# A fused AdaLN block on one core: the pass over x written out as a software pipeline on every engine

## The chip, the core and the metric

The kernel runs on one core of a Trainium2 chip. The metric is the device time of one execution in microseconds. A core has five engines that run beside each other, each with its own queue that it works through in order: TensorE (PE, matrix products, with its weight loads shown as PEld), VectorE (DVE), ScalarE (ACT), GpSimd (POOL) and SyncE (SP), which here issues nearly all DMAs. Engines wait for each other through semaphores. An instruction that waits at the head of a queue holds all that stands behind it on that engine.

## What is computed

With x of shape (2, 2048, 1024), and a modulation vector of six parts (sa, ca, ga, sb, cb, gb) for each of the two batch rows:

```
h = layernorm(x) * (1 + ca) + sa
q = h with the 2048 tokens as the reduced axis; for each of the 1024 channels l:
    scores[n, m] = sum over tokens of h[n, token, l] * h[m, token, l] / sqrt(2048)   (2 x 2)
    msg = softmax(scores) @ q
x = x + ga * (h + msg)
h = layernorm(x) * (1 + cb) + sb
x = x + gb * (silu(h @ Wg.T) * (h @ Wu.T)) @ Wd.T        (1024 -> 2752 -> 1024)
```

The modulation is silu(c) @ wmod with wmod of 1024 x 6144. Since the scores need sums over all 2048 tokens, the whole of x must be read once before the first token can go on: that reading is the pass over x that is changed here. With z = (x - mean) * r, where r is one over the standard deviation, the pass forms for each channel the five sums of z0, z1, z0², z1² and z0·z1 (0 and 1 are the batch rows).

## The kernel before

**The stages.** (1) The pass over x: eight sections of 256 tokens, both batch rows. (2) A short stage in which the sums become the 2 x 2 softmax and the modulation parts 2 to 4 are formed. (3) Eight units of 256 tokens each, which redo the normalisation for their tokens and run the feed-forward network. The products of stage 3 are split into f16 high and low parts.

**A section in the pass.** A section has four blocks of 128 tokens x 1024 channels, block (n, c) for batch row n and token half c. `x_load` (line 232) brings each row's two blocks by one DMA of 1 MB. There are eight such places in SBUF, so section s + 4 goes where section s was, and its load waits until all readers of section s are done. `x_stats` (line 245) runs `bn_stats` on half blocks and `bn_aggr` per block on DVE (lines 255 and 256), a square root on ACT (line 122), five small dependent DVE instructions (lines 125 to 128 and 261), and writes the columns r/D and nb/D of row 0 into `lw`, a weight tile of PE (line 263; nb = -mean·r, D = 1024). `x_sums` (line 287) forms z of row 1 (block c = 0 on GpSimd, line 296, and c = 1 on ACT, line 294), takes row 0 straight from x with `lw` as the weights, has the squares done by ACT (lines 315 and 316) and the mixed product by GpSimd (line 312), and adds everything up in the PSUM tile `sums` by fp32 products of 32 columns (line 299). Because row 0 is not centred in the mixed product, a product with a column of ones (`one`, line 325) corrects it. Each `add` call has a column group of 32; four of them, with four different groups, run beside each other on PE.

**Beside the sections.** For section 0, z of both rows is kept in `z_first` (in the tile `H`), and `x_turn` (line 274) transposes x and z of section 0 on PE, block of 128 channels by block, through the PSUM tile `pz`, with the copies out of PSUM taken in turn by ACT (line 285) and DVE (line 283). Parts 0 and 1 of the modulation are formed by `section_of` (line 193): four loads of 1 MB, sixteen products (line 167), a copy on ACT (line 173), four small turning products (line 176), and a copy on DVE (line 183).

**What sets the order.** Only SP is in the order of the program text (line 1036). On PE, DVE, ACT and GpSimd a list scheduler chooses the order in each queue from modelled costs; all waits between engines follow from the data. In the queues that it built, the eight `x_turn` copies of z stand among the sums of sections 0 to 2, and the statistics of a section run one to two sections ahead of its sums. After the pass, `srow` (line 1079) copies the sums out and four products `pq` (line 1081) turn them.

Of the kernel before, what the change touches and what calls it, by code (L numbers as in the profile page):

```python
# [8 lines left out]
F32 = mybir.dt.float32  # L9
F16 = mybir.dt.float16  # L10
# [7 lines left out]
P = 128  # L18
# [29 lines left out]
def adaln_kernel(ctx, tc, x, xT, wgp, wg20, wgl, wd, wd20, wd21, wmod, cT, out, nunits=NU):  # L48
# [11 lines left out]
    def ct(shape, name, dt=F32):  # L60
        return const.tile(shape, dt, tag=name, name=name)
# [13 lines left out]
    def xtile(u):  # L75
        return big[:, u % 2].rearrange("p (k n c) -> p k n c", k=KB, n=2)
# [5 lines left out]
    pick = ct([P, 34], "pick")  # L82
    V.memset(pick, 0.0)
    V.memset(pick[:, 2:3], 1.0 / D)
    one = ct([P, 1], "one")
    V.memset(one, 1.0)
    epst = ct([P, 1], "epst")
    V.memset(epst, EPS)

# [29 lines left out]
    def rsqrt(dst, v, shape, pool, tag):  # L119

        s = pool if tag is None else pool.tile(shape, F32, tag=tag, name=tag + "s")
        first = S.activation(s, v, AF.Sqrt, bias=epst)
        n = shape[-1]
        for o in range(0, n, P):
            V.reciprocal(dst[:, o:min(n, o + P)], s[:, o:min(n, o + P)])
        V.scalar_tensor_tensor(s, v, EPS, dst, ALU.add, ALU.mult)
        V.scalar_tensor_tensor(s, s, -0.5, dst, ALU.mult, ALU.mult)
        return first, V.scalar_tensor_tensor(dst, s, 1.5, dst, ALU.add, ALU.mult)
# [29 lines left out]
    def mod_load(j, kk, slots):  # L158
        wm = slots[kk % len(slots)]
        last_load[0] = Q.dma_start(wm, wmod[2 * kk * P:(2 * kk + 2) * P, j * D:(j + 1) * D].rearrange("(k p) e -> p k e", p=P))  # L160
        return wm

    def mod_mul(pm, kk, wm):
        for i in range(2):
            for h in range(2):
                o = 32 * (2 * i + h)
                last = T.matmul(pm[o:o + 32], csT[:, 2 * kk + i], wm[:, i, h * 512:(h + 1) * 512],
                                start=kk == 0, stop=kk == KB // 2 - 1, skip_group_check=True)
        return last

    def mod_end(j, pm, tag):
        row = evp.tile([P, 512], F32, tag="ev", name=f"row{j}", bufs=3)
        S.copy(row, pm)
        pt = ps.tile([P, KB // 2, 2, 2], F32, tag=tag, name=f"pt{j}")
        for k in range(KB // 2):
            mark["turn", j] = T.matmul(pt[:, k], row[:, k * P:(k + 1) * P], sel, start=k == 0, stop=k == KB // 2 - 1,
                                       skip_group_check=True)
        m = mods[j] = ct([P, KB, 2], f"mod{j}")
        m = m.rearrange("p (h k) n -> p k h n", h=2)
        if j == 4:  # L180
            V.tensor_single_scalar(m, pt, 1.0, ALU.add)
        else:
            V.tensor_copy(m, pt)
# [9 lines left out]
    def section_of(j, wms, tag, after=None):  # L193

        pm = ps.tile([P, 512], F32, tag=tag, name=f"pm{j}")
        for kk, wm in enumerate(wms):
            with tc.issue_after(after[kk].ins) if after else ExitStack():
                mod_mul(pm, kk, wm)
        mod_end(j, pm, tag)
# [16 lines left out]
    stat = dr.tile([NU, 2, 2, TU], F32, tag="stat", name="stat")  # L216
    mods = {}
    NC = TU // P
    toks = ct([P, NU, 2, 2, NC], "toks")


# [4 lines left out]
    def z_tiles(s):  # L226
        return x_tiles(s) if s else z_first

    def x_tiles(s):
        return [xnat[(2 * s + n) % len(xnat)] for n in range(2)]  # L230

    def x_load(s):
        for n in range(2):
            Q.dma_start(x_tiles(s)[n], x[n, s * TU:(s + 1) * TU, :].rearrange("(c p) e -> p c e", p=P))

    lw = tmp.tile([P, 2 * TU], F32, tag="acc", name="lw", bufs=1)[:, 0:4 * NC * 34]
    V.memset(lw, 0.0)
    lw = lw.rearrange("p (b w c e) -> p b w c e", b=2, w=2, c=NC)  # L240
    V.memset(lw[:, :, 1, :, 0:1], 1.0 / D)
    nbs = ct([P, 2, 2, NC], "nbs")
    zz_at = [hpf, bct.rearrange("p a n c -> p (a n c)")]

    def x_stats(s):
        xs = x_tiles(s)
        tok = toks[:, s]

        st4 = ps.tile([P, 3 * 2 * NC], F32, tag="X", name="st4")
        mv = st4[:, 0:4 * NC].rearrange("p (n c t) -> p n c t", n=2, c=NC)  # L250
        for n in range(2):
            for c in range(NC):
                st = small.tile([P, 2, 6], F32, tag="bst", name="bst")
                for h in range(2):
                    V.bn_stats(out=st[:, h, :], in_=xs[n][:, c, h * 512:(h + 1) * 512])
                V.bn_aggr(out=mv[:, n, c, :], in_=st)
        r = tok[:, 0].rearrange("p n c -> p (n c)")
        mean, var = (mv.rearrange("p n c t -> p (n c) t")[:, :, t] for t in range(2))
        rsqrt(r, var, [P, 2 * NC], st4[:, 4 * NC:], None)
        nb = nbs[:, s % 2].rearrange("p n c -> p (n c)")  # L260
        V.scalar_tensor_tensor(nb, mean, -1.0, r, ALU.mult, ALU.mult)
        for w, t in enumerate((r, nb)):
            V.tensor_single_scalar(lw[:, s % 2, w, :, 2], t[:, 0:NC], 1.0 / D, ALU.mult)
        V.tensor_single_scalar(tok[:, 1].rearrange("p n c -> p (n c)"), mean, -1.0, ALU.mult)

    def stat_rows():
        n = NU * 4 * NC
# [3 lines left out]
        S.copy(rows, p16[0:n, :])  # L271
        S.dma_start(stat.rearrange("s w n (c p) -> (s w n c) p", p=P), rows)

    def x_turn(dst, src):

        for k in range(KB):
            pz = ps.tile([P, 2, NC, P], F32, tag="Z", name="pz")
            for n in range(2):
                for c in range(NC):
                    T.transpose(pz[:, n, c], src[n][:, c, k * P:(k + 1) * P], ident)  # L280
            d = dst[:, k].rearrange("p n (c t) -> p n c t", c=NC)
            if k % 2:
                V.tensor_copy(d, pz)
            else:
                S.copy(d, pz)

    def x_sums(s):

        xs, zs = x_tiles(s), z_tiles(s)
        tok, nb, lws = toks[:, s], nbs[:, s % 2], lw[:, s % 2]  # L290

        def z_of(n, c):
            if c:
                S.activation(zs[n][:, c], xs[n][:, c], AF.Identity, scale=tok[:, 0, n, c:c + 1], bias=nb[:, n, c:c + 1])
            else:
                G.tensor_scalar(zs[n][:, c], xs[n][:, c], tok[:, 0, n, c:c + 1], nb[:, n, c:c + 1], ALU.mult, ALU.add)

        def add(g, w, src, first=False):
            mark["sums", s] = T.matmul(sums_ps[32 * g:32 * g + 32], w, src, start=first, stop=s == NU - 1,  # L299
                                       skip_group_check=True)  # L300

        for c in range(NC):
            z_of(1, c)
        if s == 0:
            for c in range(NC):
                z_of(0, c)
        zq = {}
        half = lambda t, h: t[:, h * 512:(h + 1) * 512]
        for c in range(NC):
            x0, z1 = xs[0][:, c], zs[1][:, c]  # L310
            zz = zz_at[c]
            G.tensor_tensor(zz, x0, z1, ALU.mult)
            for n in range(2):
                zq[n] = wp.tile([P, 2 * KH * P], F16, tag="w", name="zq").bitcast(F32)[:, 0:D]
            S.activation(zq[0], x0, AF.Square, scale=tok[:, 0, 0, c:c + 1], bias=nb[:, 0, c:c + 1])
            S.activation(zq[1], z1, AF.Square)
            for h in range(2):
                add(h, lws[:, 0, c, 2:34], half(x0, h), s == 0 and c == 0)
            for h in range(2):
                add(2 + h, lws[:, 1, c, 0:32], half(z1, h), s == 0 and c == 0)  # L320
            for n in range(2):
                for h in range(2):
                    add(2 * n + h, pick[:, 1:33], half(zq[n], h))
            for h in range(2):
                add(h, lws[:, 1, c, 2:34], one.broadcast_to([P, 512]))
            for h in range(2):
                add(2 + h, lws[:, 0, c, 0:32], half(zz, h))


    s_gu = ct([P, NP + 2], "s_gu")  # L330
# [703 lines left out]
    pairs = {0: Pair(0, four(H[:, 12:20].rearrange("p a n c -> p (a n c)")))}  # L1034
    in_order = ExitStack()
    in_order.enter_context(tc.manual_schedule(engines={mybir.EngineType.SP}))
    for g in range(4):
        x_load(g)
    wms = [mod_load(0, kk, slots[0:4]) for kk in range(4)]
    x_stats(0)  # L1040
    x_turn(xtile(0), x_tiles(0))
    x_stats(1)
    x_sums(0)
    x_load(4)
    x_turn(zt, z_first)
    for g in range(1, NU):
        if g + 1 < NU:
            x_stats(g + 1)
        x_sums(g)
        if g + 4 < NU:  # L1050
            x_load(g + 4)
        if g == 1:
            section_of(0, wms, "Z")
            wms = [mod_load(1, kk, slots[0:4]) for kk in range(4)]
        if g == 3:
            section_of(1, wms, "Z")
    stat_rows()


# [134 lines left out]
```

## Time and profile before

| | |
|---|---|
| median of 3 runs | 2642.22 us (2641.72 to 2643.38) |
| the profiled execution, own time | 2644.62 us |
| its span in the trace | 2642.8 us |
| PE busy over the span | 2570.5 us, 97% |
| DVE, ACT, POOL busy | 1593.3, 977.2, 125.9 us |
| first transposition on PE | at 9.67 us |
| `pq`, first product after the pass | at 98.48 us |
| PE busy, stretch 168 to 200 and 200 to 300 us | 32.00 of 32.00 and 100.00 of 100.00 us |

Times inside the trace are counted from the start of the span. In a list of instructions a row gives start, duration, engine, line, operation, output <- input, shape and count, and in square brackets how long the engine was idle before it and what ended that idle time. In a table of stretches a row gives the stretch, its length, each engine's busy time (with the number of instructions), the granted TensorE clock as a share of full speed, the DMA share and GB/s.

### The profile page before, as it was taken

How to read it: one execution, taken by the hardware profiler on the slowest of the kernel's cores; microseconds unless marked ns; L12 is line 12 of the kernel's file. 1: busy time of each engine (PE TensorE's matmuls, PEld its weight loads, DVE VectorE, ACT ScalarE, POOL GpSimd, SP SyncE). 2: the span in 40 equal slices, each digit the busy share in tenths (PEclk: the TensorE clock that was granted, in tenths of full speed). 3: DMA queues.
4: the chain of work that ended last, by engine and by line, in shares of the span. 5: the costliest groups of instructions: out<-in, count | busy, mean ns of one | idle time of the engine just before them, and what ended most of it. 6: DMA issues, size and time to landing. Idle time of an engine off the chain costs nothing.

```text
span 2642.8 us, 50765 instructions
## 1 busy us (share of the span) xinstructions
PE 2570.5 (97%) x21737; PEld 2089.9 (79%) x21737; DVE 1593.3 (60%) x2666; ACT 977.2 (37%) x1488; POOL 125.9 (5%) x71
## 2 busy tenths in 40 slices
PE   7899989999999999999999999999999999999999
PEld 2344448778888888878887888878887888888887
DVE  7567779866684877584384725684284824622263
ACT  5666764433441454243241423333142412311130
POOL 4311100000000000000000000000000000000000
PEclk8899999999999999999999999999999999999999
DMA  8978775565567776576666666566666666556664
GB/s 320 356 281 305 295 276 192 199 221 198 170 204 268 262 250 205 194 236 201 186 218 217 212 200 199 198 237 201 192 208 208 218 200 202 200 194 201 202 200 152
DMA packets 159011, 586.62 MB, mean 222 GB/s; under 512 B 17217, under 2 KB 17281, under 8 KB 158785
## 3 DMA queue, kind: packets, MB, share of 16 engines
q1 hardware_dynamic: 158704, 583.35, 64.8%
q8 instruction: 170, 2.79, 0.4%
q14 instruction: 57, 0.46, 0.1%
q10 hardware_dynamic: 80, 0.03, 0.0%
HBM read 506.47 MB, written 76.84 MB: 221 GB/s over the span
## 4 chain that ended last, share of the span: by engine, by line
PE 78%; DMA 9%; DVE 7%; ACT 3%; issue 2%; SPq 0%; POOL 0%; DVEq 0%; ACTq 0%; POOLq 0%
PE pY L790 19%; PE pZ L790 12%; PE pX L790 12%; PE dY L994 11%; PE dX L994 8%; PE dZ L994 7%; PE pB L1020 2%; PE g L758 2%; PE sums L299 2%; PE pl L828 1%; DMA wo<-dgu 1%; DMA out_dram<-big 1%; ACT junk L117 1%; DMA rot<-in_wgp_dram 1%; PE g L733 1%
## 5 line engine op out<-in xcount | busy, mean ns | idle before, releaser
L790 PEld LDWEIGHTS <-w 128*128 128x128 f16 x8820 | 860.7, 98 | 108.4 <-DMA w<-dgu 4.9
L994 PEld LDWEIGHTS <-wd 128*128 128x128 f16 x6720 | 657.8, 98 | 84.1 <-DMA wd<-dwd 4.0
L790 PE MATMUL pY<-hbt,w 128*128 128x256 f16 x3780 | 442.4, 273 | 0.0
L994 PE MATMUL dY<-rot,wd 128*128 128x256 f16 x2880 | 320.3, 274 | 0.0
L790 PE MATMUL pX<-hbt,w 128*128 128x256 f16 x2520 | 300.6, 273 | 0.0
L790 PE MATMUL pZ<-hbt,w 128*128 128x256 f16 x2520 | 294.5, 273 | 3.8 <-DMA w<-dgu 3.7
L790 PEld LDWEIGHTS <-wo 128*128 128x128 f16 x2688 | 263.4, 98 | 41.1 <-DMA wo<-dgu 5.6
L134 ACT ACTIVATE rot<-H,sA 128x1024 f16<-128x1024 f32 (+1 forms) x168 | 162.7, 1001 | 238.1 <-PE dY L994 129.8
L135 DVE SCALAR_TENSOR_TENSOR rot<-H,sA,rot 128x1024 f16<-128x1024 f32 (+1 forms) x168 | 182.1, 1099 | 78.2 <-ACT rot L134 77.9
L733 PE MATMUL g<-hbt,wq 128*128 128x512 f16 x1008 | 221.0, 379 | 1.8 <-ACT hbt L675 1.2
L994 PE MATMUL dX<-rot,wd 128*128 128x256 f16 x1920 | 212.9, 273 | 6.0 <-DMA wd<-dwd 3.7
L994 PE MATMUL dZ<-rot,wd 128*128 128x256 f16 x1920 | 213.5, 273 | 0.0
L807 DVE TENSOR_TENSOR ev<-pY,e 128x512 f32<-128x512 f32 (+1 forms) x72 | 47.8, 663 | 254.7 <-PE pY L790 253.6
L733 PEld LDWEIGHTS <-wq 128*128 128x128 f16 x1008 | 98.2, 98 | 119.8 <-issue 2.5
L117 ACT ACTIVATE junk<-H 128x1024 bf16<-128x1024 f32 (+1 forms) x100 | 98.7, 987 | 161.9 <-DVE H L817 143.7
L812 ACT ACTIVATE sil<-ev,inv_f 128x512 f32<-128x512 f32 (+1 forms) x72 | 50.5, 701 | 246.3 <-DVE ev L810 246.1
L790 PE MATMUL pY<-hbt,wo 128*128 128x256 f16 x1152 | 135.2, 273 | 3.6 <-DVE ev L807 2.6
L587 ACT ACTIVATE o<-big,beta,alpha 128x256 f32<-128x256 f32 x112 | 59.9, 591 | 207.2 <-DVE big L573 183.6
L798 DVE TENSOR_TENSOR ev<-pY,e 128x512 f32<-128x512 f32 (+1 forms) x72 | 47.7, 662 | 124.1 <-PE pY L790 124.1
L758 PE MATMUL g<-hbt,wo 128*128 128x256 f16 x960 | 108.3, 275 | 3.3 <-DMA wo<-dgu 3.1
L801 ACT COPY e<-pZ 128x512 f32<-128x512 f32 (+1 forms) x72 | 40.3, 560 | 188.5 <-PE pZ L790 188.5
L758 PEld LDWEIGHTS <-wo 128*128 128x128 f16 x960 | 94.4, 99 | 16.2 <-DMA wo<-dgu 3.3
(291 smaller groups left out, 2763.7 us busy)
## 6 DMA issues: line engine op xcount, KB each, us to landing
w<-dgu SPq DMA_DIRECT2D x350, 512.0 KB, 4.2
wd<-dwd SPq DMA_DIRECT2D x224, 640.0 KB, 4.0
wo<-dgu SPq DMA_DIRECT2D x85, 512.0 KB, 5.4
dgu<-wo SPq DMA_DIRECT2D x40, 512.0 KB, 4.0
rot<-in_wgp_dram SPq DMA_DIRECT2D x38, 512.0 KB, 5.8
dgu<-wq SPq DMA_DIRECT2D x35, 512.0 KB, 6.6
big<-in_wgp_dram SPq DMA_DIRECT2D x32, 512.0 KB, 7.5
out_dram<-big SPq DMA_DIRECT2D x30, 512.0 KB, 3.1
```

What stands on the lines that cost most here:

```text
L117: S.activation(jv, src, AF.Square, accum_out=col)
L134: mark["hi"] = S.activation(dst_hi, src, AF.Copy, scale=s)
L135: return V.scalar_tensor_tensor(dst_lo, src, s, dst_hi, ALU.mult, ALU.subtract)
L299: mark["sums", s] = T.matmul(sums_ps[32 * g:32 * g + 32], w, src, start=first, stop=s == NU - 1, skip_group_check=True)
L587: S.activation(o[:, n], z[:, q, 0], AF.Identity, scale=alpha[:, n, 0, q:q + 1], bias=beta[:, n, q:q + 1])
L733: T.matmul(pt[m, f].rearrange("p n c -> p (n c)"), w[:, wa, f, k], hb0[:, ha, 4 * kh + k], start=kh == 0 and k == 0 and j == 0, stop=kh == ...
L758: T.matmul(pt[m, f][:, n], w[:, wa, f, k], hb[:, ((1, 0), (2, 3))[kh][n], ha, k], start=kh == 0 and k == 0 and j == 0 and n == 0, stop=kh ...
L790: T.matmul(pt[a][:, f], w[:, wa, f, k], hb[:, i, ha, k], start=a not in seen, stop=k == 3 and j == 2, skip_group_check=True)
L807: V.tensor_tensor(c22, pt["Y"], e1, ALU.add)
L812: S.activation(sr, u2, AF.Silu, scale=inv)
L994: T.matmul(acc[a, h][:, j], w[:, k // 5, wa, k % 5], rot16[:, si % 2, ha, k], start=(a, h) not in seen, stop=k == KH - 1 and jj == 2, skip ...
L1020: T.matmul(pB, wt[0:n, k, wa, m, :], hp[0:n, k, ha, :], start=i == 0, stop=i == len(LAST) - 1)
```

## The change

1. z is formed for all four blocks of every section: block (0, 0) on DVE, (1, 0) on GpSimd, (0, 1) and (1, 1) on ACT. All sums then have plain z, z² or z·z as data and the constant `pick` as weights. The tile `lw` and its DVE writes, `one` and its products are gone: 20 products per section in place of 24.
2. PE, DVE, ACT and GpSimd are put in the order of the program text for the whole pass (`in_text`). The text is written as a pipeline: step s (`x_step`) holds the statistics of section s + 1 around the z of section s.
3. The transposition of x of section 0 has all eight copies on ACT, ahead of the first square root. The transposition of z is spread out: one channel block after the sums of each of the steps 1 to 7, its copy on ACT after odd steps and on DVE after even ones, and the eighth after the last step.
4. The loads of modulation parts 0 and 1 are issued in halves between the loads of x, and their products stand in halves behind the sums of steps 2 and 3 (part 0) and 5 and 6 (part 1).

The diff, cut to its core (`stats` keeps the `bn_stats` and `bn_aggr` of one row; `root` is the square root on ACT; `squares` two squares on ACT):

```diff
-        for w, t in enumerate((r, nb)):
-            V.tensor_single_scalar(lw[:, s % 2, w, :, 2], t[:, 0:NC], 1.0 / D, ALU.mult)
...
+    def dev(s):
+        mean, v, r = parts(s)
+        d = toks[:, s, 0].rearrange("p n c -> p (n c)")
+        V.reciprocal(d, r)
+        V.scalar_tensor_tensor(r, v, EPS, d, ALU.add, ALU.mult)
+        V.scalar_tensor_tensor(r, r, -0.5, d, ALU.mult, ALU.mult)
+        V.scalar_tensor_tensor(d, r, 1.5, d, ALU.add, ALU.mult)
+        V.scalar_tensor_tensor(nbs[:, s % 2].rearrange("p n c -> p (n c)"), mean, -1.0, d, ALU.mult, ALU.mult)
+        V.tensor_single_scalar(toks[:, s, 1].rearrange("p n c -> p (n c)"), mean, -1.0, ALU.mult)
+
+    def z_of(E, s, n, c):
+        src, dst = x_tiles(s)[n][:, c], z_tiles(s)[n][:, c]
+        r, nb = toks[:, s, 0, n, c:c + 1], nbs[:, s % 2, n, c:c + 1]
+        if E is S:
+            S.activation(dst, src, AF.Identity, scale=r, bias=nb)
+        else:
+            E.tensor_scalar(dst, src, r, nb, ALU.mult, ALU.add)
...
+    def x_turn(dst, src, k, E):
+        pz = ps.tile([P, 2, NC, P], F32, tag="Z", name="pz")
+        for n in range(2):
+            for c in range(NC):
+                T.transpose(pz[:, n, c], src[n][:, c, k * P:(k + 1) * P], ident)
+        d = dst[:, k].rearrange("p n (c t) -> p n c t", c=NC)
+        S.copy(d, pz) if E is S else V.tensor_copy(d, pz)
...
+    def x_step(s):
+        z = [[z_tiles(s)[n][:, c] for n in range(2)] for c in range(NC)]
...
+        if more:
+            stats(s + 1, 0)
+        dev(s)
+        z_of(V, s, 0, 0)
+        if more:
+            stats(s + 1, 1)
+        z_of(G, s, 1, 0)
+        for n in range(2):
+            z_of(S, s, n, 1)
+        for c in range(NC):
+            G.tensor_tensor(zz_at[c], z[c][0], z[c][1], ALU.mult)
+        zq = squares(s, 0)
+        if more:
+            root(s + 1)
+        zq += squares(s, 1)
+        for c in range(NC):
+            for n in range(2):
+                add(s, 0, 2 * n, z[c][n])
+        for n in range(2):
+            add(s, 1, 2 * n, zq[n])
+        for c in range(NC):
+            add(s, 2, 2 * c, zz_at[c])
+        for n in range(2):
+            add(s, 1, 2 * n, zq[2 + n])
...
+    in_text.enter_context(tc.manual_schedule(engines={getattr(mybir.EngineType, e) for e in ENGINES}))
     for g in range(4):
         x_load(g)
-    wms = [mod_load(0, kk, slots[0:4]) for kk in range(4)]
-    x_stats(0)
-    x_turn(xtile(0), x_tiles(0))
...
+    w0 = [mod_load(0, kk, slots[0:4]) for kk in range(2)]
+    stats(0, 0)
+    stats(0, 1)
+    for k in range(KB):
+        x_turn(xtile(0), x_tiles(0), k, S)
+    root(0)
+    for g in range(NU):
+        x_step(g)
         if g + 4 < NU:
             x_load(g + 4)
+        if g == 0:
+            w0 += [mod_load(0, kk, slots[0:4]) for kk in (2, 3)]
+        if g == 2:
+            pm0 = ps.tile([P, 512], F32, tag="st", name="pm0")
+            for kk in range(2):
+                mod_mul(pm0, kk, w0[kk])
+            w1 = [mod_load(1, kk, slots[0:4]) for kk in range(2)]
+        if g == 3:
+            for kk in (2, 3):
+                mod_mul(pm0, kk, w0[kk])
+            mod_end(0, pm0, "st")
+            w1 += [mod_load(1, kk, slots[0:4]) for kk in (2, 3)]
...
+        if g:
+            x_turn(zt, z_first, g - 1, S if g % 2 else V)
+    x_turn(zt, z_first, KB - 1, V)
+    in_text.close()
     stat_rows()
```

Steps 5 and 6 do for part 1 what steps 2 and 3 do for part 0.

## The prediction

> **What bounds the kernel now.** I read the stretches first: from 168 us on PE is busy without a break, so nothing later can take back what the start loses or gains; and of the time that PE waits between 100 and 340 us none goes to a DMA (6.6 us on GpSimd, the rest on ACT and DVE). So a shift of the first product after the pass (`pq`, 98.48 us) goes into the end time one to one. I then followed the chain of waits through the pass:
>
> ```profile
> 74.28 3.47 PE sums L299 x34
> 77.75 1.00 PE pt L176 x8
> ...
> 82.17 7.40 PE sums L299 x32
> ...
> 93.36 4.33 PE sums L299 x42
> 97.69 0.86 PE pm L167 x8
> 98.55 0.99 PE pq L1081 x8
> ```
>
> From 41 us to the end the chain is PE's queue itself, with one break at 78 to 82. Before 41 us it is DVE. What an engine does when its next instruction is not ready shows in DVE's own order of time:
>
> ```profile
> 35.45 1.73 DVE L263 TENSOR_SCALAR lw<-nbs 128x2 f32<-128x2 f32 x1
> 37.10 2.39 DVE L263 TENSOR_SCALAR lw<-toks 128x2 f32<-128x2 f32 x1
> ...
> 42.99 0.16 DVE L261 SCALAR_TENSOR_TENSOR nbs<-st,toks 128x4 f32<-128x4 f32 x1
> 47.65 0.17 DVE L263 TENSOR_SCALAR lw<-toks 128x2 f32<-128x2 f32 x1 [4.50 <-PE sums L299]
> ```
>
> Two things: a write of two elements took 2.39 us while GpSimd ran its 2.34 us product (37.13), against 0.16 elsewhere; and one DVE instruction that needed PE's sums held the whole DVE queue 4.50 us. The second is what I expect of the change. The durations for the sum, by operation, in the pass (mean ns behind the busy time):
>
> ```profile
> L255 DVE BATCH_NORM_STATS2 bst<-hbt 128x6 f32<-128x512 f32 x32 | 19.6, 669 | 0.0
> L312 POOL TENSOR_TENSOR hp<-hbt 128x1024 f32<-128x1024 f32 x3 | 7.2, 2385 | 0.1
> ...
> L316 ACT ACTIVATE zq<-hbt 128x1024 f32<-128x1024 f32 x6 | 6.3, 1043 | 0.0
> ...
> L294 ACT ACTIVATE hbt<-hbt,nbs,toks 128x1024 f32<-128x1024 f32 x3 | 3.7, 1234 | 1.8 <-DVE nbs L261 1.8
> L296 POOL TENSOR_SCALAR hbt<-hbt,toks,nbs 128x1024 f32<-128x1024 f32 x3 | 3.6, 1200 | 3.5 <-DVE lw L263 2.0 <-DVE toks L264 1.6
> ```
>
> Back to back, ACT starts one every 1.13 (z) and 0.95 (square), and DVE a `bn_stats` every 0.60. PE starts eight records, four products in four groups, at 47.40 and the next eight at 48.26: 0.86 a group of four.
>
> **What is removed.** 24 products a section become 20, six groups of four become five: 8 x 0.86 = 6.9 us of PE. The 16 writes of L263 go, 9.9 us of DVE with their blocking. Both are gains only if those engines stay the bound. **What is added:** a z on DVE each section, and seven more on ACT (7 x 1.13, on an engine idle for 45 of the first 100 us: free). The DMAs are the same; x of section 4 is asked for right after the z of section 0, near 24 us in place of 30.67. In the slower pass below loads are ahead by 10 us or more everywhere, so the halved loads cost and bring nothing; the 4.0 us that DVE waited for x at 69 us go.
>
> **The new order.** Per step, from the moment `dev` (the five dependent DVE instructions, 84.63 to 85.68, with the next 1.1) is done:
> - DVE: z of block (0, 0), then half of the next statistics, 4 x 0.60 + 2 x 0.2 + hand-offs = 2.9, then the other half, 2.9, then `dev`, 1.1. The z is not in the trace. Upper bound 1.2, as two-input operations on 1024 elements (L366, 1.22); lower bound 0.6, half of that, as the blocking of L263 behind GpSimd hints that the form uses a second port. I take 0.9, next to the 0.91 of the only DVE row with 1024 fp32 results and no such input (a memset, L496). Period 0.9 + 2.9 + 2.9 + 1.1 = **7.8**.
> - GpSimd: z 1.2 after DVE's, then two products of 2.4: done at 6.9. ACT: two z, two squares, root 0.2, two squares: done at 6.4. PE then has the second mixed product and the last squares, two half-overlapping pairs, 1.6: sums done at **8.5**.
>
> Sums of step s end 8.5 after `dev`, later than DVE's 3.8 for the statistics that it does before the next half section. That is harmless until something on DVE waits for what stands behind the sums on PE. The text puts just that there: after steps 2, 4 and 6 DVE's copy of the transposed z, and after steps 3 and 6 the copy of the modulation part. Behind the waiting copy stand the next statistics (2.9) and `dev` (1.1), and for `dev` all four engines wait. By step, from `dev` to the next `dev`:
> - Steps 0, 1, 5: 7.8 each. After 1 and 5 the copy is on ACT; it ends 9.8 and 11.6 after `dev` (5 has two groups of products, 1.7, ahead), so ACT starts the next step 2.0 and 3.8 late.
> - Step 2: ACT late by 2.0, sums at 9.3; products 1.7; transpositions 0.6 (4 at L280); copy 0.7 (L283); hand-offs 0.2: 12.5. Then 2.9 + 1.1: **16.5**.
> - Step 3: 8.5 + products 1.7 + copy on ACT 0.6 (L173) + turning 1.0 (L176) + copy 0.2 + hand-offs 0.3 = 12.3, + 4.0: **16.3**.
> - Step 4: 8.5 + 0.6 + 0.7 + 0.1 + 4.0 = **13.9**.
> - Step 6: ACT late by 3.8, sums at 11.1; 1.7 + 0.6 + 1.0 + 0.3, transpositions 0.6, copy 0.7 with small DVE work: 16.1, + 1.1: **17.2**.
> - Step 7: 8.5.
>
> The first `dev`: eight copies on ACT in a row, two `pz` buffers, about 0.9 each with transpositions of 1.1 at the low clock, from 11.2 to 18.3; table load 1.28, root 0.24, `dev` 1.1: 20.8 (before 23.1). Sum: 20.8 + 3 x 7.8 + 16.5 + 16.3 + 13.9 + 17.2 + 8.5 = **116.6**.
>
> **The clock.** PE's granted clock (third number from the end of a row; PE's busy time is the second) falls after thin stretches:
>
> ```profile
> 16.50:20.00 3.50, 1.97 (x8) 1.43 (x8) 3.49 (x12) 0.56 (x1) 0.00 (x0) 0.50 1.03 412
> 20.00:23.40 3.40, 1.38 (x6) 0.71 (x4) 3.40 (x13) 0.67 (x2) 0.01 (x1) 0.50 1.02 408
> 23.40:26.70 3.30, 3.29 (x8) 0.41 (x8) 3.27 (x10) 3.30 (x3) 3.30 (x3) 0.51 1.03 408
> 26.70:30.00 3.30, 3.30 (x32) 2.17 (x34) 3.30 (x10) 3.30 (x6) 3.30 (x2) 1.00 1.02 407
> ...
> 36.80:40.10 3.30, 0.01 (x1) 0.00 (x0) 3.30 (x4) 3.30 (x4) 2.66 (x2) 1.00 0.61 245
> 40.10:43.50 3.40, 3.36 (x16) 1.24 (x20) 1.87 (x8) 2.30 (x5) 0.00 (x0) 0.52 0.00 1
> ```
>
> A stretch with PE busy 56% left it at 0.50, one full stretch brought it back, an idle one lost it. Each long step leaves PE idle 4 us or more, so the next one starts at half clock; its first groups have room (they wait for GpSimd and ACT anyway), so I count half of a second 0.86 + 0.6 in each of four steps: 4 x 0.75 = 3.0. Sums end at 119.6, against 97.7 before: **+21.9**.
>
> **After the pass.** Two transpositions now stand ahead of `pq`: 1.2 + 0.2 after the sums against 0.8, +0.6. All 16 products of modulation part 2 follow `pq` (before 8), and on ACT the two table loads precede the copy of its row: `beta` 8.3 after the start of `pq` against 7.6, +0.7. Together **+23.2**. The profiled execution, 2644.62, would be 2667.8; it lies 2.4 above the median 2642.22, so I name **2665.4**.
>
> Two rules of the Trainium skill weigh on this and change no number above. VectorE: DVE Perf Modes, Mode 2×_2P, says that a one-input fp32 operation within SBUF does two elements a cycle; no row here shows it, and by it z takes about 0.6 (an estimate from that page), the sum 2.4 us less. SBUF — State Buffer, Who interferes with whom, says that the first of DVE and GpSimd to start holds the shared ports for its whole instruction. The L263 rows show that at 2.39 us, and it speaks against a z on DVE; but GpSimd is done at 6.9, before the next z at 7.8, and the sum stays. If GpSimd were late, up to 2.4 for each of three short steps.
>
> **Rivals.**
> - *The pipeline runs at DVE's pace, faster.* If the copies found PE ready, or the wait cost only the copy, the pass is 20.8 + 7 x 7.8 + 5 small copies 2.5 + 8.5 = 86.4, -11.3 + 1.3 = -10: 2632. It decides at 3.8 us after `dev`: PE would have to be done with the sums by then. For it: DVE is the bound until 41 us, PE loses 6.9 us of work. Against: GpSimd alone needs 6.0 of the 8.5.
> - *Half clock throughout.* If no step has a full stretch, groups cost 1.72 and the sums of a step end at 10.4 (five groups from 1.0 on, and hand-offs). Step 2 then grows by 5.5 (sums 3.3 with ACT later by 2.4, products 1.7, transpositions 0.5), step 3 by 4.5 (1.9, 1.7, turning 0.9), step 4 by 2.4, step 6 by 8.1 (sums 5.0 with ACT later by 4.1), step 7 by 1.9: +22.4 in place of 3.0: 2685. Against: at half clock the work fills a stretch, which brought the clock back at 26.70.
> - *Nothing shows.* DMA or the later stages absorb it: 2642 to 2647. Against: no DMA wait of PE, PE full from 168.
>
> **Numbers.** Forecast case 0.82, pace of DVE 0.09, half clock 0.07, nothing 0.02. Low end: no clock cost (-3), z 0.6 (-2.4), GpSimd's z not behind DVE's (-3): 2657, I set 2656. High end: z 1.2 (+2.4), clock double (+3), ports (+7): 2678. A measurement of this kernel can tell about 0.2% from no change: faster 0.09, same 0.02, slower 0.89.
>
> **What would show it.** Right: DVE idle 5 to 9 us before the copies after steps 2, 3, 4, 6, with PE's `pz` or `pt` as the ender; `pq` near 120; `dev` 8 us apart in steps 0, 1 and 5. Wrong: no such idle time, `pq` before 95, or z on DVE over 2 us.

## The result, and the profile after

The changed kernel takes 2665.74 us (median of four runs, 2662.32 to 2671.26), against 2642.39 before (2641.72 to 2643.38): 1.009 times as long, with a 95% interval of 1.0072 to 1.0108. The profiled execution took 2665.11, with a span of 2663.3 (before 2644.62 and 2642.8). The forecast was 2665.4.

The pass is where it was lost. `pq`, the first product behind it, starts at 114.74 us in place of 98.48. DVE's rows in order of time show the waits (start, duration, engine, line and operation; in brackets the idle time ahead and who ended it):

```profile
46.39 0.69 DVE L292 COPY big<-pz 128x512 f32<-128x512 f32 x1 [8.37 <-PE pz L290]
47.00 1.28 DVE L247 BATCH_NORM_STATS2 bst<-hbt 128x6 f32<-128x512 f32 x2
...
50.88 0.81 DVE L275 TENSOR_SCALAR rot<-rot,toks,nbs 128x1024 f32<-128x1024 f32 x1
51.61 1.28 DVE L247 BATCH_NORM_STATS2 bst<-hbt 128x6 f32<-128x512 f32 x2
...
63.18 0.18 DVE L181 COPY mod<-pt 128x16 f32<-128x16 f32 x1 [8.64 <-PE pt L174]
...
76.35 0.69 DVE L292 COPY big<-pz 128x512 f32<-128x512 f32 x1 [5.54 <-PE pz L290]
...
103.13 0.18 DVE L181 COPY mod<-pt 128x16 f32<-128x16 f32 x1 [11.23 <-PE pt L174]
```

Four copies of 0.18 and 0.69 us each stand behind 5.5 to 11.2 us of idle time. Behind the copies stand statistics that need nothing of PE: in the first experiment below, where the copy is not in front of them, the two `bn_stats` that stand at 47.00 here run at 37.47 (its row is shown there). Where no copy waits, DVE runs without a gap (50.88 to 54.54).

The chain of waits, which follows the end time back, runs through one such loop (start, duration, what):

```profile
59.68 1.74 PE pm L165 x14
61.45 0.59 ACT row L171
62.09 1.07 PE pt L174 x8
63.35 1.19 DVE bst L247 x2
64.80 1.15 DVE bst L247 x2
65.97 0.22 DVE st L248
67.23 0.80 POOL hbt L275
...
71.38 2.39 POOL bct L325
73.82 1.91 PE sums L296 x12
75.73 0.60 PE pz L290 x4
76.35 0.69 DVE big L292
```

Before, from 41 us on, the chain was PE's queue with one break. Now one step's products, copy, statistics, `dev`, z, mixed product and sums stand one behind the other, each on an engine while the others wait. PE is busy 10.72 of the 20 us from 60 to 80 (before 18.74).

### The profile page after: what moved, and what is told of

The parts are those of the page before. It is cut to its first block, busy times and chain, and to the rows that moved or that the text cites. A ratio compares the mean times of both kernels' runs of the same rounds, so it can differ in the third digit from the quotient of the medians.

```text
span 2663.3 us, 50633 instructions
## 1 busy us (share of the span) xinstructions
PE 2575.6 (97%) x21673; PEld 2090.5 (78%) x21673; DVE 1588.5 (60%) x2651; ACT 984.8 (37%) x1499; POOL 132.4 (5%) x70
## 4 chain that ended last, share of the span: by engine, by line
PE 82%; DMA 6%; DVE 6%; ACT 3%; issue 2%; POOL 1%; SPq 0%; DVEq 0%; POOLq 0%; ACTq 0%
PE pY L801 19%; PE pZ L801 12%; PE pX L801 12%; PE dY L1005 11%; PE dX L1005 8%; PE dZ L1005 7%; PE g L744 3%; PE g L769 3%; PE pB L1031 3%; PE pl L839 1%; DMA wo<-dgu 1%; ACT junk L115 1%; DMA wl<-dgl 1%; PE sums L296 1%; DMA rot<-in_wgp_dram 1%
## 5 line engine op out<-in xcount | busy, mean ns | idle before, releaser
L823 ACT ACTIVATE sil<-ev,inv_f 128x512 f32<-128x512 f32 (+1 forms) x72 | 50.4, 700 | 242.5 <-DVE ev L821 242.3
L769 PEld LDWEIGHTS <-wo 128*128 128x128 f16 x960 | 94.4, 99 | 17.1 <-DMA wo<-dgu 4.7
```

The source lines that it names most:

```text
L769: T.matmul(pt[m, f][:, n], w[:, wa, f, k], hb[:, ((1, 0), (2, 3))[kh][n], ha, k], start=kh == 0 and k == 0 and j == 0 and n == 0, stop=kh ...
L823: S.activation(sr, u2, AF.Silu, scale=inv)
```

## The experiments

A period is the distance from one `dev` to the next, by the start of its write of `nbs` (L266 in the changed kernel). In the changed kernel: the first `dev` at 19.4, then periods of 7.3, 7.4, 16.5, 16.3, 13.7, 7.4, 17.1; the sums end 8.5 after the last `dev` is done.

### DVE's copies one step later

```diff
-        S.copy(d, pz) if E is S else V.tensor_copy(d, pz)
+        if E is S:
+            S.copy(d, pz)
+        else:
+            late.append(lambda: V.tensor_copy(d, pz))
...
-            V.tensor_copy(m, pt)
+            late.append(lambda: V.tensor_copy(m, pt)) if j < 2 else V.tensor_copy(m, pt)
...
         if more:
             stats(s + 1, 1)
+        while late:
+            late.pop(0)()
...
```

> All five waiting copies of DVE in the pass (transposed z after steps 2, 4 and 6, modulation part after steps 3 and 6) are issued one step later, behind the second half of the next section's statistics; PE, ACT and GpSimd keep their order. Queue theory (a waiting copy holds the next statistics and dev): the periods of 16.5, 16.3, 13.7 and 17.1 fall to 7.4 to 11 (ACT's own copies still hold it for 2 to 4 us), pq starts near 89 in place of 114.7, the time falls by about 25 to 2640 (2633 to 2647). Rival, PE at half clock sets the long steps: the sums keep their pace, under 8 us are gained, 2658 to 2666. Rival, DVE's z beside GpSimd's (shared port) and the added work on ACT: the copies cost only their own 0.2 and 0.7, under 4 us gained, 2661 or more.

Measured: 1.0001 of before (0.999 to 1.0012), 2641.31; the periods are 7.3, 7.4, 7.8, 8.8, 9.9, 8.0, 8.9, and `pq` starts at 91.75. So 23.0 us of the pass were waits of five copies whose own work is 2.4 us, and the time follows: from 1.009 to 1.0001 of 2642 is 23.5 us. The statistics of the step now run first, and the copy that waited 8.37 us waits 0.60:

```profile
37.47 1.23 DVE L248 BATCH_NORM_STATS2 bst<-hbt 128x6 f32<-128x512 f32 x2
...
45.94 0.69 DVE L296 COPY big<-pz 128x512 f32<-128x512 f32 x1 [0.60 <-PE pz L291]
```

The rival "ports" is out as the cause of the long steps: DVE's z still runs beside GpSimd's, whose row is 1.73 here too. Half clock is not excluded by this run alone, since PE also waits less in it; it is tested by itself below. What holds the longer of the remaining periods is ACT's queue, by the same mechanism:

```profile
52.11 0.58 ACT L172 COPY row<-pm 128x512 f32<-128x512 f32 x1 [3.42 <-PE pm L166]
54.34 0.59 ACT L294 COPY big<-pz 128x512 f32<-128x512 f32 x1 [1.64 <-PE pz L291]
54.82 2.37 ACT L274 ACTIVATE hbt<-hbt,nbs,toks 128x1024 f32<-128x1024 f32 x2
```

Two copies wait for PE, and z, which could have started at 50.4, starts at 54.82. DVE's rows show the end of it: `dev` waits 2.28 us at 59.23 for ACT's root.

### One half of it at a time

The first kernel puts only the `tensor_copy(d, pz)` a step later, the second only the `tensor_copy(m, pt)`.

> Only the transposed-z copies after steps 2, 4 and 6 are issued one step later; the modulation copies after steps 3 and 6 stay where they wait. Queue theory: steps 2 and 4 shrink to 7.4 to 8.5, step 3 stays at 16, step 6 stays above 14; 15 us gained, pq near 99, time near 2650 (2645 to 2655). Half clock or ports: under 5 us, above 2660.

> Only the modulation copies after steps 3 and 6 are issued one step later; the transposed-z copies stay. Queue theory: step 3 falls from 16.3 to about 8, but ACT's copy of the row then reaches into step 4, whose own wait grows (13.7 to about 18), and step 6 still waits for its z copy (13 to 16): only about 5 us gained, pq near 110, time near 2661 (2656 to 2664). If each wait were simply a cost of its own, half of all, 12 or more, would go: 2653 or less.

Measured: the transposed z alone, 1.0018 (1.0009 to 1.0028), 2646.51, `pq` at 98.49; the modulation copies alone, 1.0071 (1.0054 to 1.0088), 2661.80, `pq` at 110.94. Against 114.74 that is 16.3 and 3.8 us; together they gave 23.0. The 3.8 is the instructive number. Step 3 fell from 16.3 to 7.4, but step 4 grew from 13.7 to 18.2:

```profile
63.37 0.17 DVE L182 COPY mod<-pt 128x16 f32<-128x16 f32 x1 [1.00 <-PE pt L175]
...
72.37 0.69 DVE L293 COPY big<-pz 128x512 f32<-128x512 f32 x1 [8.62 <-PE pz L291]
...
99.82 0.69 DVE L293 COPY big<-pz 128x512 f32<-128x512 f32 x1 [11.90 <-PE pz L291]
```

About half of the wait of 8.64 was passed on: DVE came to the next copy 7.1 us sooner, but PE had its transposition done only 4.0 sooner. In step 6 all of it was: the copy of the transposed z, which stands right behind, now waits 11.90 where the modulation copy waited 11.23, and the period is 17.2 where it was 17.1. A wait at the head of a queue is worth its length only if no later one takes it over.

### The changed arithmetic in the scheduler's order

The line that puts PE, DVE, ACT and GpSimd into the order of the text is left out; SP keeps its order.

> The changed arithmetic (z of both rows, 20 products a section, z on DVE, halved loads), but PE, DVE, ACT and GpSimd in the scheduler's order, as before the change; only SP stays in the written order. Queue theory: the written order is the cause, not the arithmetic; where the scheduler puts DVE's copies behind statistics the long steps shrink, pq between 88 and 100 and the time 2636 to 2650. If the arithmetic (z on DVE beside GpSimd, two more operations a section on ACT) or the halved loads were the cause, the time stays above 2658.

Measured: 0.9989 of before (0.9979 to 0.9998), 2638.74; `pq` at 89.42. The arithmetic of the change, with its z on DVE and its halved loads, ends the pass 9.1 us sooner than before; the written order takes that and 16.3 more. In the scheduler's order the copies of DVE stand behind other statistics, though not all: waits of 1.1 to 9.7 us are left.

### Nothing waits for its own step

ACT's copies go a step later too, behind the next step's two z; the turning of a modulation row on PE goes behind the next step's sums. (The column of ones is kept in this one; its part is told below.)

```diff
...
+            late_act.append(lambda: S.copy(d, pz))
...
         for n in range(2):
             z_of(S, s, n, 1)
+        run(late_act)
...
         for n in range(2):
             add(s, 1, 2 * n, zq[2 + n])
+        run(late_pe)
...
+        late_act.append(lambda: S.copy(row, pm))
+        late_pe.append(turn)
...
```

> As the last one, and ACT's waiting copies (transposed z, the row of a modulation part) are issued in the next step too, behind its two z; the turning of the row on PE follows the next step's sums, its copy on DVE comes a step later still. Queue theory: nothing in a queue waits for the sums of its own step, so every period is DVE's 7.4 to 8.2, the last dev at 72 to 76, pq at 82 to 86, and the time 2626 to 2630. If PE's half clock or GpSimd bounds the steps by then, periods stay at 9 or more and the time above 2633.

Measured: 0.9971 of before (0.9958 to 0.9985), 2637.50 beside 2643.9 in the same runs. It has the lowest ratio of all versions and is faster than both kernels, though its interval overlaps that of the scheduler's order (0.9979 to 0.9998). The pass is as expected: periods of 7.3, 7.4, 7.4, 8.0, 7.4, 8.2, 6.5, `pq` at 83.22. The copy that waited 8.37 us now finds its data there:

```profile
45.39 0.22 DVE L266 BATCH_NORM_AGGREGATE st<-bst 128x2 f32<-128x12 f32 x1
45.52 0.67 DVE L313 COPY big<-pz 128x512 f32<-128x512 f32 x1
46.11 1.27 DVE L265 BATCH_NORM_STATS2 bst<-hbt 128x6 f32<-128x512 f32 x2
```

The time was expected at 2626 to 2630 and missed that: a pass that ends 15.3 us sooner gave 7.7 (0.9971 of 2642). The experiments on the rest of the shift, below, look for the difference.

### The clock

Five products of 128x512 that nobody reads are put on PE behind steps 2, 3, 4 and 6, where it would wait.

```diff
+    def x_warm():
+        held.append(ps.tile([P, 2, NC, P], F32, tag="Z", name="pz"))
+        for _ in range(5):
+            T.matmul(held[0].rearrange("p n c t -> p (n c t)"), ident, big[:, 0, 0:512], start=True, stop=True)
...
+        if g in (2, 3, 4, 6):
+            x_warm()
```

> The changed kernel with five products of 128x512 that nobody reads, put on PE behind steps 2, 3, 4 and 6, where it waits 4 us or more, so that it does not fall to half clock there. The clock term of the prediction (3.0 us in four steps): pq near 112, time 3 us less, 2662. My reading of the changed kernel's trace: the periods of the long steps are as worked out without that term, since the groups at half clock wait for GpSimd and ACT anyway; pq stays within 1 us of 114.7 (or goes up, where the added products run at half clock themselves), time 2664 to 2668.

Measured: `pq` at 114.47, 1.0082 of before (1.0063 to 1.01); as the changed kernel. The fill did what it should to the clock. The same stretch of step 3 in both (busy time of PE, PEld, DVE, ACT and GpSimd, granted clock, DMA share, GB/s), first the changed kernel:

```profile
53.50:56.90 3.40, 3.40 (x22) 1.23 (x18) 1.00 (x3) 3.40 (x5) 3.40 (x2) 0.50 0.32 127
```

then with PE filled:

```profile
53.50:56.90 3.40, 2.70 (x20) 0.42 (x14) 0.94 (x3) 3.40 (x5) 3.40 (x2) 1.00 0.29 116
```

From 46.6 to 114.6 us every stretch of 3.4 us is granted 1.00 there, where the changed kernel has 0.50 to 0.66 in seven of twenty and 0.83 to 0.86 in four more. It is worth 0.3 us of `pq`. ACT and GpSimd are full in that stretch of both: PE's slow groups lie beside the squares and mixed products that the sums wait for anyway.

### Where the rest of the shift goes

The prediction took a shift of the pass one to one to the end. I compared when PE starts the small products of the scale factors (`pa`, L93 in the changed kernel, L95 before), which stand in the same order in all kernels. Up to 399 us the shift stays; behind, it grows: for the changed kernel +16.65 at 134 us, +15.64 at 399, +18.36 at 717, +20.48 at 2551. Six more kernels look for the cause.

First the place. The column of ones (4 bytes, removed by the change) takes 32 bytes in each partition, so the ring of weight tiles starts at byte 203,296 in place of 203,328. One kernel keeps the column in the changed kernel, one adds a second column to the kernel before, and one keeps it in the kernel with DVE's late copies.

```diff
+    one = ct([P, 1], "one")
+    V.memset(one, 1.0)
```

> The changed kernel with the unused column of ones kept (its tile and its memset), so that everything allocated behind it stands where it stood before the change: the ring of weight tiles at byte 203,328 of a partition (a multiple of 64) in place of 203,296 (32 over). The pass itself is as in the changed kernel, pq at 114.7. So far the five profiles of the changed arithmetic keep their shift at pq up to 400 us, and by the medians all cost 5 to 7 us more behind it, with DMA engines busy 0.65 to 0.67 of the stretches behind 1350 us against 0.62 to 0.64 before, for the same bytes. Place theory (the weight stream writes to a place that is 32 bytes off costs DMA time): that share falls to 0.62 to 0.64 and the time by about 6, to 2660 (2657 to 2662). Rival, the late growth comes from the later start or from the halved loads: 2665, share 0.66.

> The kernel before the change with one more column of 4 bytes allocated beside the column of ones, and nothing else: the ring of weight tiles moves from byte 203,328 to 203,360 (32 over a multiple of 64). Place theory: 5 to 7 us slower, 2647 to 2649, DMA share behind 1350 us 0.65 to 0.67. Rival (start or loads): 2642, share 0.63.

> The kernel with DVE's copies one step later, and the column of ones kept. Queue theory and place theory together: pq at 91.8, 6.7 before that of the kernel before, and nothing given back behind: 2635 (2633 to 2637). If the place does nothing: 2641.

Measured: 1.0077 (1.0063 to 1.0092), 0.9997 (0.9988 to 1.0006) and 1.0005 (0.9995 to 1.0015). The place theory falls: moving the ring costs the kernel before nothing, and putting it back brings the late copies nothing and the changed kernel nothing that its interval lets one see. Its other leg falls too: the moved kernel's DMA share between 1350 and 2550 us is 0.64 to 0.66, where the kernel before has 0.62 to 0.64, and its time is the same.

Then the loads and the start. The changed arithmetic in the scheduler's order gets whole loads; the kernel before gets a later start, by fills of the first section's place that its load must wait for. That load now also stands behind those of sections 1 to 3 and of modulation part 0.

```diff
-    for g in range(4):
+    for g in range(1, 4):
         x_load(g)
...
+    for _ in range(10):
+        V.memset(x_tiles(0)[0], 0.0)
+    x_load(0)
```

> The changed arithmetic in the scheduler's order, with the loads of the modulation sections whole and the two sections in one piece after steps 1 and 3, as before the change. The prediction gave the halved loads no cost and no gain: pq at 87 to 92 and the time within 3 us of the same with halved loads (2638.7, 0.9989 of before). If the halving is what costs 3 to 8 us behind 400 us, the time falls to 0.997 of before or less.

> The kernel before the change, with x of section 0 asked for only when DVE has filled its place ten times (some 18 us of added work, which the load then overwrites); the other loads go out first as before. The pass is a translation of the old one by 12 to 17 us, with the old arithmetic and order. If the end follows the pass one to one, as the prediction says, the time grows by just the shift of pq. Measured so far: with the changed arithmetic, by the medians, the time is 3 to 8 us more than the shift at 400 us. If that comes from any start that has another distance to the loads, it shows here too: 4 us or more above the shift. If it belongs to the changed pass, the time is within 2 us of the shift.

> As the delayed kernel before, with two fills of the first section's place in place of ten: x of section 0 is asked for near 13 us, and pq should move by -1 to +5 us. Every start so far that differs from the old one, with old or changed arithmetic, costs 3 to 8 us behind 400 us on top of its shift, by the medians; the same start with everything behind it moved by 32 bytes costs nothing. If the old start is a lucky one, this one pays too: 3 us or more above its shift of pq. If only shifts of 6 us or more pay, the time is within 2 us of the shift.

Measured: whole loads 1.0008 (0.9997 to 1.0019), `pq` at 95.41; ten fills 1.0082 (1.0069 to 1.0095), `pq` at 116.05; two fills 1.0056 (1.0043 to 1.0069), `pq` at 111.77, 13.3 later where I expected -1 to +5. With two fills the load goes out at 13.97, but DVE waits for it until 32.32: it is the place behind the other loads that delays it. So this kernel does not test a small shift. Nor is either a pure translation of the pass, as their first `dev` comes 22.4 and 26.5 later and `pq` only 13.3 and 17.6. The halved loads show no cost: with whole ones the pass is 6.0 us longer and the time 1.0008 in place of 0.9989, though there the modulation products stand elsewhere too. For every kernel, the ratio times 2642 less the shift of `pq` from 98.48:

| kernel | shift of `pq` | time by the ratio | behind the pass |
|---|---|---|---|
| before, ring moved | -1.2 | -0.8 | +0.4 |
| before, two fills | +13.3 | +14.8 | +1.5 |
| before, ten fills | +17.6 | +21.7 | +4.1 |
| z copies late | 0.0 | +4.8 | +4.8 |
| whole loads, scheduler's order | -3.1 | +2.1 | +5.2 |
| late copies | -6.7 | +0.3 | +7.0 |
| late copies, column kept | -6.0 | +1.3 | +7.3 |
| scheduler's order | -9.1 | -2.9 | +6.2 |
| nothing waits | -15.3 | -7.7 | +7.6 |
| mod copies late | +12.5 | +18.8 | +6.3 |
| changed, PE filled | +16.0 | +21.7 | +5.7 |
| changed, column kept | +16.2 | +20.3 | +4.2 |
| changed | +16.3 | +23.8 | +7.5 |

Each ratio is known to 2 to 5 us, and each `pq` comes from one profile (pairs that differ only in the column are 0.1 to 1.2 apart), so no row says much alone. The base is one profile too: with 97.27 for it, as with the ring moved, every row would be 1.2 lower. But all ten kernels with the changed pass lose 4 to 8 us behind it, whether it ends sooner or later, and the three with the old pass 0 to 4. Neither order, nor halved loads, nor 32 bytes explains that. What all ten share was not taken apart: the changed arithmetic itself, and that with the tile `lw` gone the three tiles `o` and the tile `acc`, which the later stages use, change places. The granted clock gives no lead: in stretches of 300 us from 400 to 2500 us it reads 0.98, 0.99 and then 1.00 in both kernels, though one hundredth of a stretch is 3 us. What the profiles show of the loss is PE waiting for weights and for what is made of them. Of the changed kernel behind 400 us, the waits of PE (engine, line, who was waited for: us in total, times, longest):

```profile
PE pl L839 <- DMA wl<-dgl: 5.5, 4, 3.4
PE dX L1005 <- DMA wd<-dwd: 4.1, 1, 4.1
PE g L769 <- DMA wo<-dgu: 3.8, 2, 3.2
PE pX L801 <- DMA wo<-dgu: 3.7, 2, 3.6
PE pZ L801 <- DMA w<-dgu: 3.6, 2, 2.3
```

All such waits sum to 28.9 us, against 25.3 in the kernel before. Over the profiles they are 23.7 to 28.8 in four with the old pass and 25.6 to 31.3 in ten with the changed one: 2.8 us between their means, where the means of the table's two groups are 4.2 apart (6.2 and 2.0). That is too scattered for more. The cause stays open.

## Why the prediction held, and where it did not

**The mechanism** is shown, by removing it: DVE's queue, held by copies that wait for what stands behind PE's sums. Of its four long steps (16.5, 16.3, 13.9, 17.2) the trace has 16.5, 16.3, 13.7 and 17.1; the idle times, the enders (`pz`, `pt`) and the 8.5 us from the last `dev` to the end of the sums are those that were named.

**The size of the pass** was not right. The sums were put at 119.6 and end at 113.9:
- The first `dev` is done 1.2 us sooner: ACT's eight copies end at 16.88, not 18.3.
- The short steps are 7.38, not 7.8, three times 0.42: z and the halves of the statistics follow one another more closely. z takes 0.81, inside the bounds 0.6 and 1.2 and next to the 0.9 taken.
- The long steps together are 0.3 less.
- **The clock term, 3.0, is the step that failed.** The text counted "half of a second 0.86 + 0.6 in each of four steps". With PE at full clock throughout, `pq` moves by 0.3, so the term is worth 0.3 and not 3.0: those groups lie beside GpSimd's and ACT's work.

**After the pass**, +1.3 was forecast, and some 0.5 came: the sums end 16.2 later than before, `pq` starts 16.26 and `beta` (the last small DVE result ahead of the next stage) is done 16.65 later. That the halved loads "cost and bring nothing" is not confirmed either: the version with whole loads is the slower one, by 6.0 at `pq`. But that was measured in the scheduler's order, and its modulation products stand elsewhere. As forecast, DVE waits for no load in the changed pass.

**"A shift goes into the end time one to one"** holds to 399 us (+15.64) and, for the changed pass, no further. The forecast had nothing behind that; the profile has +4.8 there. So 2665.4 against 2665.74 is partly luck. Up to `beta` the forecast was 6.6 too high (23.2 against 16.65), behind it 3.8 too low (the spans differ by 20.5), and the remaining 2.8 is the place of the two profiled executions among their runs: 2.2 above the median before, 0.6 below it after. The argument from "PE is full from 168 us" shows that nothing absorbs a shift, but not that the rest keeps its length: in the profiles PE still waits 24 to 31 us behind 400 us.

**The ports.** DVE's z does lengthen GpSimd's beside it: GpSimd's row in the changed kernel is 1.73 where it was 1.20.

```profile
50.95 1.73 POOL L275 TENSOR_SCALAR rot<-rot,toks,nbs 128x1024 f32<-128x1024 f32 x1 [9.49 <-DVE toks L267]
52.76 2.38 POOL L325 TENSOR_TENSOR hp<-rot 128x1024 f32<-128x1024 f32 x1
55.10 2.37 POOL L325 TENSOR_TENSOR bct<-rot 128x1024 f32<-128x1024 f32 x1
```

GpSimd starts 0.07 after DVE's z (50.88) and needs 0.53 more than in the kernel before, yet is done 6.6 after `dev`, sooner than the 6.9 taken. The kernel in the scheduler's order shows that z is the cause: there GpSimd's z takes 1.19 to 1.20 where no z of DVE lies beside it and 1.63 to 1.74 where one does.

The Trainium skill, SBUF — State Buffer, Who interferes with whom, says of DVE in a two-port mode that the first of the two to start holds the shared ports for its whole instruction. The rows agree in kind, but 0.53 is less than the 0.74 that was left of z, and the recorded starts do not always tell who waits. The write of L263 that took 2.39 began at 37.10, 0.03 ahead of the GpSimd product beside it. In the scheduler's order a z of DVE that began at 67.00, 0.07 ahead of a GpSimd product of 2.39, took 3.01 in place of 0.81. So the cost that was feared from the ports exists; in the written order, where DVE's z always comes beside GpSimd's z and not beside its products, it does not arise.

The Trainium skill's VectorE: DVE Perf Modes, Mode 2×_2P, gave about 0.6 for z (the prediction's estimate from that page). The row's 0.81, or 0.73 from its start to that of the next instruction, decides.

**The rival "at DVE's pace, faster"** needed copies that find PE ready. The kernel in which nothing waits for its own step is that rival: the pass takes the pace of DVE, `pq` at 83.2 (it was put at about 87), and the time falls by 7.7 (0.9971 of 2642) where 10 was given. The pass itself ends 15.3 sooner; the difference lies behind it.

## What to carry to other kernels

In a written order, look at each engine's queue for the first instruction that needs the result of the step's last engine, and at what is ready behind it; issue such a copy a step later, where its data are old. Do this on every queue at once: if only some waiting copies are moved, the next one can take over their waits (of 8.64 and 11.23 us moved, 3.8 were gained). A forecast made from one stage should carry an error for the stages behind it even if they are full.

## What was not expected of the hardware

- PE's half clock cost the pass nothing that shows: granted 0.50 to 0.66 in seven of twenty stretches, or 1.00 in all, `pq` came within 0.3 us.
- GpSimd's z, started 0.07 after DVE's, took 0.53 us longer than in the kernel before, less than the 0.81 of DVE's z. By L263 before the change I had feared 2.4, and beside a GpSimd product, in the scheduler's order, DVE's z did take 3.01.
- In the best version the loads run at 408 GB/s with a DMA share of 1.03 from 20 to 80 us; in the changed kernel they fall to 289 between 60 and 80. I read that as loads that wait for places which the held pass frees late. The trace fits, as SP's loads of x wait 19.9 us for PE's sums there between 20 and 110 us (12.0 in the best version between 20 and 90), but no run isolates it.
